# An RWKV block with FP4 feed-forward: the fifth branch's small products move beside two others, GpSimd's sums are split, and tiles are written in place

## Chip, cores, metric

One core of one Trainium2 chip. The metric is the device time of the kernel in microseconds, the median of three runs. The engines are TensorE (PE; its weight loads are PEld), VectorE (DVE), ScalarE (ACT), GpSimd (POOL), and SyncE (SP), which issues the DMAs.

## What is computed

The input is x of shape (2, 4096, 256), float32. A modulation vector gives scales, shifts and gates per batch. A layer norm with modulation leads into a two-layer RWKV-6 stack; its output, gated, is added to x; a second modulated layer norm leads into a feed-forward network with FP4-quantized weights and activations, gated and added again. The part that the change touches is the time mix of each layer:

```python
sx = _shift(x) - x
xxx = x + sx * p['x_maa']
mix = jnp.tanh(xxx @ p['tm_w1']).reshape(b * t, 5, E)                            # E = 32
mix = jnp.einsum('nfe,fed->fnd', mix, p['tm_w2']).reshape(5, b, t, d)
mw, mk, mv, mr, mg = mix
wx = x + sx * (p['w_maa'] + mw)     # and so for k, v, r and g
r = sigmoid(rx @ Wr); k = kx @ Wk; v = vx @ Wv; g = silu(gx @ Wg)
w = exp(-exp(time_decay + tanh(wx @ td_w1) @ td_w2))
# per head: out_t = r_t (S + u k_t v_t^T);  S = diag(w_t) S + k_t v_t^T
x = x + (groupnorm(out) * g) @ Wo
```

A channel mix follows (a shift, two interpolations, a squared ReLU and a sigmoid gate).

## The kernel before

**Tiles and steps.** All work is float32; a matmul of that type is two records in the trace, each with its own weight load. Time is cut into blocks of 256 positions. A step is one block of one batch in one layer: 2 batches x 2 layers x 16 blocks = 64 steps. Each (batch, layer) is a stream, a Python generator; the feed-forward's inputs, its chunks, its weights and the modulation are streams too.

**The planner.** The streams do not issue instructions. They record them with the class `Plan`, which simulates the five engines with a cost for each instruction and picks, again and again, the recorded instruction that could start first (with preferences for older work and for TensorE products that keep the array's form). What it picks is issued, so the order of every engine's queue is that of the plan, and the engines wait for each other by semaphores only. `Plan.after` says when a result is seen by the next engine: `LAT` of the producer plus `SEEN` of the consumer (55 ns for TensorE, 80 for GpSimd, 35 otherwise), or `SAME` on the same engine. `start` demands that all the PSUM banks that a group of products needs are free together; there are five banks, and the oldest group that still needs banks keeps as many from the others. The last lines of the kernel function make the plan for each of `PLANS` seeds (a jitter of the ages) without issuing, and then issue the one with the least planned end.

**Memory.** Work tiles come from stocks: `SLOTS` tiles of 514 floats per partition, `SLOTS2` double tiles of 1024 for the recurrence's r and k, `LONG` tiles of 768 for the feed-forward. A stream takes a tile from a stock and gives it back when it has recorded the last reader.

**Time mix.** `shifted` normalizes, transposes to channels by TensorE, scales into a second tile with one more column at the front (the last position of the block before), and lets GpSimd form the difference sx. The first product gives 128 rows for the branches w, k, v, r (32 each) and 128 more rows that hold the fifth branch's 32 rows four times, since the weights are laid out so. The second products have a contraction of 32: a product on rows 0 to 31 of the partitions uses row group 0 of the array, rows 32 to 63 group 1, and so on. The fifth branch uses groups 0 and 1, one for each block of 128 output channels, in two banks; then `branch_pair(0, 3)` (w and r) uses groups 0 and 3, and later `branch_pair(1, 2)` (k and v) groups 1 and 2. `to_input` empties a bank by two VectorE instructions, (product + maa) * sx, and one GpSimd sum adds x to the whole tile.

**The recurrence** (`wkv`) works on two chunks of 128 positions by seven levels of doubling. One stream at a time may record it (`head_lock`). It first writes copies of r and k, with the bonus u on even or odd positions, into two slots, for level 0; each level multiplies parts of r and k in place by products of the decays (`pair_view`).

Of the kernel before, what the change touches and what calls it, by code (L numbers as in the profile page):

```python
# [25 lines left out]
E = 32  # L26
# [11 lines left out]
TURNS = 30.0  # L38
SLOTS = 36
STAGGER = (12, 60)  # L40
PLANS, JITTER = 8, 8.0
SLOTS2 = 4
TINY = 16
LONG = 5
AHEAD_OPS = 24
# [72 lines left out]
class Plan:  # L118
# [10 lines left out]

    LAT = {"tensor": 170.0, "vector": 0.0, "scalar": 0.0, "gpsimd": 0.0, "sync": 2600.0, "load": 0.0}  # L130


    LAP = {"vector": 84.0, "scalar": 100.0, "gpsimd": 40.0}
    SEEN = {"tensor": 55.0, "gpsimd": 80.0}
    SAME = {"vector": 34.0, "scalar": 25.0, "gpsimd": 80.0}

# [323 lines left out]
def rwkv_adaln_fp4_kernel(ctx: ExitStack, tc: tile.TileContext, a: dict, out: bass.AP):  # L460
# [129 lines left out]
    for i in range(L):  # L590
        w = {}
        small = wp.tile([P, SMALL], F32, name=f"small{i}")
        load(small, a["small"][i])
        for n, v in enumerate(VECS):
            w[v] = small[:, n * J : (n + 1) * J]
        at = len(VECS) * J
        w["w1"] = small[:, at : at + J * 8 * E].rearrange("p (k n) -> p k n", k=J)
        at += J * 8 * E
        w["td1"] = small[:, at : at + J * ED].rearrange("p (k n) -> p k n", k=J)
        at += J * ED  # L600
        w2a, w["w2b"], w["td2"] = (small[:, at + m * D : at + (m + 1) * D] for m in range(3))
        w["w2"] = [w2a[E * f : E * (f + 1), :] for f in range(4)]
        for n in ("Wr", "Wk", "Wv", "Wg", "Wo"):
            w[n] = load_mat(f"{n}_{i}", a["L0_attn_" + n][i], J)
        w["wvm"] = const.tile([P, J * H], F32, name=f"wvm{i}")
        w["centred"] = False
        w["cWk"] = load_mat(f"cWk_{i}", a["L0_attn_cWk"][i], J)
        w["cWv"] = load_mat(f"cWv_{i}", a["L0_attn_cWv"][i], FD // P)
        w["cWr"] = load_mat(f"cWr_{i}", a["L0_attn_cWr"][i], J)
        lay.append(w)  # L610
        load_wmod(1 + i)
# [56 lines left out]
    for i in range(L):  # L668
        for b in range(B):
            nc.gpsimd.memset(state[i][b], 0.0)  # L670
            for m in range(2):
                nc.gpsimd.memset(carry[i][b][m], 0.0)
    diag = keep.tile([P, 2, C, J, 32], F32, name="diag")
    attn = keep.tile([P, 2, C, J, P], F32, name="attn")
# [83 lines left out]
    def shifted(h, ln_w, car):  # L758

        xn_s = take_slot()  # L760
        xn = v3(xn_s)
        yield from layernorm(h, xn)
        bk, pt = to_channels(xn)
        x_s = take_slot()
        xT = x_s.rearrange("p (j t) -> p j t", j=J)
        pl.vector.tensor_copy(xT[:, :, 0:1], car)
        for j in range(J):
            pl.scalar.activation(xT[:, j, 1:], pt[:, j, :], AF.Copy, scale=ln_w[:, j : j + 1])
        pl.close(bk)
        give(xn_s)  # L770
        pl.vector.tensor_copy(car, xT[:, :, TT : TT + 1])
        sx_s = take_slot()
        sx = v3(sx_s)
        pl.gpsimd.tensor_tensor(sx, xT[:, :, 0:TT], xT[:, :, 1:], ALU.subtract)
        yield
        return xT[:, :, 1:], sx, x_s, sx_s

    def lerp(x, sx, maa):
        m_s = take_slot()
        m = v3(m_s)  # L780
        for j in range(J):
            pl.vector.scalar_tensor_tensor(
                m[:, j, :], sx[:, j, :], maa[:, j : j + 1], x[:, j, :], ALU.mult, ALU.add
            )
        return m, m_s
# [18 lines left out]

    def pair_view(rk, h, n):

        v = rk[:, h : h + 1]
        return bass.AP(v.tensor, v.offset, [v.ap[0], [J * TT - h, 2], [2 * h, n], [1, h]])

# [27 lines left out]
    def wkv(i, b, rk_s, dec_s, v_s):  # L837

        S = state[i][b]
        rk = rk_s[:, : 2 * J * TT]  # L840
        r, k = (rk[:, m * J * TT : (m + 1) * J * TT].rearrange(
            "p (c j t) -> p c j t", c=C, j=J) for m in range(2))
        dec, v = v4(dec_s), v3(v_s)
        yield from take(head_lock, (i, b))
        late = pl.cur.late
        pl.cur.late = late - RUSH
        r0_s, k0_s = take_slot(), take_slot()
        r0, k0 = v4(r0_s), v4(k0_s)
        with_bonus(r0, r, 0, lay[i]["time_first"])
# [6 lines left out]
        tots_s = take_slot()  # L856
        at = 0
        def products(l):
            R, K = (r0, k0) if l == 0 else (r, k)
            wid = 64 if l == 6 else 32  # L860
# [16 lines left out]
        for l in range(7):  # L877
            h = 1 << l

            for m in {0: (), 1: (0, 1)}.get(l, (l,)):  # L880
                products(m)
            if l == 1:
                give(r0_s, k0_s)

# [3 lines left out]
            tv = tot.rearrange("p (n two) -> p n two", two=2)  # L888
            upd = pair_view(rk, h, n)
            pl.vector.tensor_tensor(  # L890
                upd, upd, tv.rearrange("p n m -> p m n").unsqueeze(3).to_broadcast([P, 2, n, h]), ALU.mult
            )
# [21 lines left out]
            yield  # L914
        give(dec_s)
        tot = tot.rearrange("p (c j) -> p c j", c=C)
        for q in range(4):
# [60 lines left out]
    def time_mix(i, b, h):  # L978
# [7 lines left out]
        for k in range(J):  # L986
            mm(pm[:, TT : 2 * TT], w["w1"][:, k, P:], xx[:, k, :], k == 0, k == J - 1)
        give(xx_s)
        mix_s = take_slot()
        mixa, mixb = mix_s[:, :TT], mix_s[:, TT : 2 * TT]  # L990
# [3 lines left out]

        def to_input(o, maa):

            m_s = take_slot()
            m = v3(m_s)
            for j in range(J):
                pl.vector.scalar_tensor_tensor(  # L1000
                    m[:, j, :], o[j], maa[:, j : j + 1], sx[:, j, :], ALU.add, ALU.mult
                )
            pl.gpsimd.tensor_tensor(m, m, x, ALU.add)
            return m_s

        def branch_pair(f, g, maa_f, maa_g):

            bks, os = zip(*(pl.bank() for _ in range(2)))
            for j in range(J):
                for e, o in zip((f, g), os):  # L1010
                    mm(
                        o[:, j * TT : (j + 1) * TT], w["w2"][e][:, j * P : (j + 1) * P],
                        mixa[E * e : E * (e + 1), :], True, True,
                    )
            ms = []
            for bk, o, maa in zip(bks, os, (maa_f, maa_g)):
                ms.append(to_input([o[:, j * TT : (j + 1) * TT] for j in range(J)], maa))
                pl.close(bk)
            return ms


        bks, os = zip(*(pl.bank() for _ in range(2)))
        for j in range(J):
            js = slice(j * E, (j + 1) * E)
            mm(os[j][:, :TT], w["w2b"][js, j * P : (j + 1) * P], mixb[js, :], True, True)
        xg_s = to_input([o[:, :TT] for o in os], w["g_maa"])
        for bk in bks:
            pl.close(bk)
        yield
        xw_s, xr_s = branch_pair(0, 3, w["w_maa"], w["r_maa"])  # L1030
        bk, pg = proj(w["Wg"], v3(xg_s))
        give(xg_s)
        g_s = take_slot()
        g_t = v3(g_s)
# [6 lines left out]
        for k in range(J):  # L1041
            for c in range(C):
# [3 lines left out]
                )  # L1046
        give(xw_s)
        td_s = take_slot()
        td = td_s[:, :P]
        pl.scalar.activation(td, pd[:, :P], AF.Tanh)  # L1050
        pl.close(bk)
        yield
        xk_s, xv_s = branch_pair(1, 2, w["k_maa"], w["v_maa"])
        give(mix_s, x_s, sx_s)
        rk_s = take_slot2()
# [31 lines left out]
        if not w["centred"]:  # L1087
# [8 lines left out]
            )  # L1096
        v_s = take_slot()
        xv = v3(xv_s)
        bk, o = proj_tok(w["Wv"], [xv[:, k, :] for k in range(J)])
        pl.scalar.copy(v3(v_s), o)  # L1100
        pl.close(bk)
        give(xv_s)
        yield

        o_s = yield from wkv(i, b, rk_s, dec_s, v_s)
        bk, pt = to_channels(v3(o_s))
        give(o_s)
        oT_s = take_slot()
        oT = v3(oT_s)
# [15 lines left out]
    def channel_mix(i, b, h):  # L1125
        w = lay[i]
        x, sx, x_s, sx_s = yield from shifted(h, w["ln2_w"], carry[i][b][1])
        xk, xk_s = lerp(x, sx, w["ck_maa"])
        xr, xr_s = lerp(x, sx, w["cr_maa"])
        give(x_s, sx_s)  # L1130
        yield
        kks = []
        for g in range(FD // P // 2):
            bk, o = pl.bank()
            o = halves(o)
            for m in range(2):
                n0 = (2 * g + m) * P
                for k in range(J):
                    mm(o[:, m, :], w["cWk"][:, k, n0 : n0 + P], xk[:, k, :], k == 0, k == J - 1)
            kks.append(take_slot())  # L1140
            kg = v3(kks[-1])
# [3 lines left out]
            yield  # L1145
        give(xk_s)
        sr_s = take_slot()
        sr = v3(sr_s)
        bk, o = proj_tok(w["cWr"], [xr[:, k, :] for k in range(J)])
        pl.scalar.activation(sr, o, AF.Sigmoid)  # L1150
        pl.close(bk)
        give(xr_s)
        yield
# [152 lines left out]
    def ffn_inputs():  # L1306
# [3 lines left out]
        for n in range(B * NT):  # L1310
# [5 lines left out]
            xn = v3(xn_s)  # L1316
            yield from layernorm_rows(x1, xn, rows["cb"][b], lambda c: rows["sb"][b])
            p_s = pl.take(long)
            yield from fp4(pl, xn_s, C * D, P, scales[0], p_s)
            long.append(p_s)  # L1320
            xq_s = take_slot()
            xqT = v3(xq_s)
            bk, pt = to_channels(xn)
            pl.scalar.copy(xqT, pt)
            pl.close(bk)
            give(xn_s)
            left = []
# [14 lines left out]
    def ffn_chunk(c, b, t, x1_s, xq_s, left):  # L1342
        HF = FI // 2
        cs_ = slice(c * P, (c + 1) * P)
        x1, xqT = v3(x1_s), v3(xq_s)
        hb_s = pl.take(long)
        hb = hb_s[:, :FI]
        for s in range(2):
# [12 lines left out]
            pl.close(bk)  # L1361
            yield
        p_s = pl.take(long)
        yield from fp4(pl, hb_s, FI, P, scales[1 + c], p_s)
        long.append(p_s)
        hT_s = pl.take(long)
        hT = hT_s.rearrange("p (f n) -> p f n", f=NF)
        for g in range(2):
# [8 lines left out]
            yield  # L1377
        long.append(hb_s)
        bk, y = pl.bank()
# [90 lines left out]
```

## Time and profile before

| | |
|---|---|
| runs of the kernel | 3128.61, 3125.28, 3124.25 us; median 3125.28 |
| profiled execution | 3123.61 us, span 3121.7 us, mean granted TensorE clock 0.981 |
| TensorE busy | 2984.9 us (96%), 38460 records |
| VectorE busy | 2365.4 us (76%) |
| ScalarE busy | 1615.4 us (52%) |
| GpSimd busy | 940.6 us (30%) |
| DMA | 42.53 MB, mean 14 GB/s |

Busy time of an engine is the time in which at least one of its instructions runs. In a group's row, the counts and shapes come first (output <- inputs, partitions x elements), then busy us and mean ns of one instruction, then the idle time of the engine just before them and what ended it. Nearly all instructions carry line 294, where the planner issues them, so groups are told apart by tiles and shapes. In the table of stretches the columns are: the stretch, its length, the busy us of PE, PEld, DVE, ACT and POOL, the granted clock, the DMA share and GB/s. In a row of waits: who waited, for whom, us in total, times, the longest.

### The profile page before, as it was taken

What the parts mean: (1) busy time and instruction counts of PE and PEld (TensorE: products, weight loads), DVE (VectorE), ACT (ScalarE), POOL (GpSimd) and SP (SyncE); (2) the same over time, 40 slices, a digit from 0 to 9 for tenths busy, and PEclk for the clock granted to TensorE, in tenths of its full rate; (3) what the DMA queues carried; (4) which work ended last, traced back from release to release, by engine and by line L of the source; (5) the groups of instructions that cost most, each with busy time, mean ns of one, the idle gap of its engine ahead of it and who ended that gap; (6) DMA issues with size and microseconds to landing.
All of it is one profiled execution on the core that took longest, in us unless ns stands there. A gap on an engine that the chain in (4) does not pass through costs nothing. (4 is left out here: it accounts for less than half of the span.)

```text
span 3121.7 us, 89338 instructions
## 1 busy us (share of the span) xinstructions
PE 2984.9 (96%) x38460; PEld 2412.9 (77%) x38460; DVE 2365.4 (76%) x6146; ACT 1615.4 (52%) x3362; POOL 940.6 (30%) x888
## 2 busy tenths in 40 slices
PE   6899999999999999999999999999999999999997
PEld 4777778778787777877778787787878778787775
DVE  6785778777877777778777787777777778766877
ACT  3565555545555556455454655546445455455442
POOL 2233323223233332332323233232332323331220
PEclk9899999999999999999999999999999999999989
DMA  4000000000000000000000000000000000000000
GB/s 141 20 14 5 10 7 15 7 15 7 9 12 7 16 8 11 11 6 17 5 11 11 5 18 5 14 8 9 13 6 17 5 8 15 9 9 9 8 13 11
DMA packets 35725, 42.53 MB, mean 14 GB/s; under 512 B 2817, under 2 KB 33537, under 8 KB 35329
## 3 DMA queue, kind: packets, MB, share of 16 engines
q1 hardware_dynamic: 35328, 36.81, 3.7%
q8 instruction: 302, 4.95, 0.7%
q14 instruction: 95, 0.77, 0.1%
HBM read 28.41 MB, written 8.39 MB: 12 GB/s over the span
## 5 line engine op out<-in xcount | busy, mean ns | idle before, releaser
L294 POOL TENSOR_TENSOR slot<-slot,slot 128x512 f32<-128x512 f32 (+1 forms) x448 | 508.9, 1152 | 961.5 <-DVE slot L294 682.0
L294 ACT ACTIVATE slot<-bank 128x512 f32<-128x512 f32 (+2 forms) x644 | 331.6, 519 | 682.8 <-PE bank L294 661.1
L294 POOL TENSOR_TENSOR tiny<-tiny,nhalf 128x2 f32<-128x2 f32 (+1 forms) x288 | 289.3, 1009 | 869.6 <-DVE tiny L294 789.4
L294 DVE TENSOR_TENSOR slot<-slot,slot 128x512 f32<-128x512 f32 x512 | 372.1, 728 | 110.2 <-PE pa L294 79.6
L294 PE MATMUL bank<-slot,small 32*128 32x256 f32 (+3 forms) x2816 | 393.3, 361 | 8.9 <-DVE slot L294 4.4
L294 PE MATMUL bank<-slot,cWk 128*128 128x256 f32 x1536 | 367.9, 385 | 2.5 <-DVE slot L294 2.0
L294 PE MATMUL bank<-cWv,slot 128*128 128x256 f32 x1536 | 343.8, 380 | 0.0
L294 PEld LDWEIGHTS pa<-slot 64*32 64x32 f32 x19456 | 224.0, 109 | 154.2 <-DVE diag L294 54.2
L294 PEld LDWEIGHTS bank<-slot,small 32*128 32x128 f32 (+3 forms) x2816 | 272.3, 178 | 88.3 <-issue 33.8
L294 PEld LDWEIGHTS bank<-slot,cWk 128*128 128x128 f32 x1536 | 284.5, 191 | 46.9 <-DVE slot L294 4.3
L294 PEld LDWEIGHTS bank<-cWv,slot 128*128 128x128 f32 x1536 | 289.2, 190 | 39.8 <-issue 0.3
L294 PE MATMUL pa<-slot 64*32 64x16 f32 x19456 | 266.2, 191 | 43.0 <-DVE diag L294 23.7
L294 ACT ACTIVATE slot<-bank,small 128x256 f32<-128x256 f32 (+1 forms) x640 | 248.4, 449 | 111.6 <-PE bank L294 109.9
L294 DVE SCALAR_TENSOR_TENSOR slot<-bank,small,slot 128x256 f32<-128x256 f32 x640 | 271.8, 473 | 24.9 <-PE bank L294 23.9
L294 DVE TENSOR_TENSOR slot<-slot,bank 128x512 f32<-128x512 f32 x192 | 131.0, 682 | 189.3 <-PE bank L294 143.0
L294 POOL TENSOR_TENSOR slot<-slot 128x512 f32<-128x512 f32 x128 | 141.9, 1111 | 346.8 <-ACT slot L294 272.3
L294 ACT ACTIVATE slot<-slot 128x512 f32<-128x512 f32 x288 | 181.3, 633 | 42.8 <-DVE slot L294 38.0
L294 DVE TENSOR_TENSOR long<-long,bank 128x352 f32<-128x352 f32 x256 | 131.1, 514 | 93.0 <-ACT long L294 69.8
L294 DVE SCALAR_TENSOR_TENSOR slot<-slot,small,slot 128x256 f32<-128x256 f32 x384 | 186.7, 518 | 16.8 <-POOL slot L294 16.7
L294 PE MATMUL bank<-ident,slot 128*128 128x128 f32 x1152 | 178.0, 283 | 14.0 <-ACT slot L294 8.6
L294 ACT COPY slot<-bank 128x512 f32<-128x512 f32 x224 | 130.3, 586 | 111.3 <-PE bank L294 107.3
L294 PE MATMUL bank<-wd,long 128*128 128x256 f32 x768 | 184.7, 391 | 1.2 <-ACT long L294 1.2
(106 smaller groups left out, 5362.5 us busy)
## 6 DMA issues: line engine op xcount, KB each, us to landing
slot<-in_L_attn_x_dram SPq DMA_DIRECT2D x64, 256.0 KB, 2.7
out_dram<-slot SPq DMA_DIRECT2D x64, 128.0 KB, 1.7
slot<-in_L_wmod_dram SPq DMA_DIRECT2D x6, 256.0 KB, 7.7
cWk<-in_L_attn_cWk_dram SPq DMA_DIRECT2D x2, 768.0 KB, 8.2
cWv<-in_L_attn_cWv_dram SPq DMA_DIRECT2D x2, 768.0 KB, 9.4
small<-in_small_dram SPq DMA_DIRECT2D x2, 718.0 KB, 8.3
long<-in_L_ffn_w_down_dram SPq DMA_DIRECT2D x2, 352.0 KB, 2.8
long<-in_L_ffn_w_gate_dram SPq DMA_DIRECT2D x5, 128.0 KB, 7.2
```

Source lines behind the costliest of these rows:

```text
L294: fn(*[real(v) for v in a], **{n: real(v) for n, v in k.items()})
```

## The change

The products: `branch_pair` becomes `branches`, which takes any number of branches and a place for each result. The fifth branch's two products use one bank and row group 1 (the second of its four copies), and stand in one group with those of w and r, in row groups 1, 0 and 3. The pair k and v stays.

```diff
-        w2a, w["w2b"], w["td2"] = (small[:, at + m * D : at + (m + 1) * D] for m in range(3))
-        w["w2"] = [w2a[E * f : E * (f + 1), :] for f in range(4)]
+        w2a, w2b, w["td2"] = (small[:, at + m * D : at + (m + 1) * D] for m in range(3))
+        w["w2"] = [w2a[E * f : E * (f + 1), :] for f in range(4)] + [w2b[E : 2 * E, :]]
...
-            pl.gpsimd.tensor_tensor(m, m, x, ALU.add)
+            for j in range(J):
+                pl.gpsimd.tensor_tensor(m[:, j, :], m[:, j, :], x[:, j, :], ALU.add)
...
-        def branch_pair(f, g, maa_f, maa_g):
-
-            bks, os = zip(*(pl.bank() for _ in range(2)))
+        def branches(es, places):
+
+            bks, os = zip(*(pl.bank() for _ in es))
             for j in range(J):
-                for e, o in zip((f, g), os):
+                for e, o in zip(es, os):
+                    rows_, mix = (slice(E * e, E * (e + 1)), mixa) if e < 4 else (slice(E, 2 * E), mixb)
                     mm(
-                        o[:, j * TT : (j + 1) * TT], w["w2"][e][:, j * P : (j + 1) * P],
-                        mixa[E * e : E * (e + 1), :], True, True,
+                        o[:, j * TT : (j + 1) * TT], w["w2"][e][:, j * P : (j + 1) * P], mix[rows_, :],
+                        True, True,
                     )
...
-        bks, os = zip(*(pl.bank() for _ in range(2)))
-        for j in range(J):
-            js = slice(j * E, (j + 1) * E)
-            mm(os[j][:, :TT], w["w2b"][js, j * P : (j + 1) * P], mixb[js, :], True, True)
-        xg_s = to_input([o[:, :TT] for o in os], w["g_maa"])
...
-        xw_s, xr_s = branch_pair(0, 3, w["w_maa"], w["r_maa"])
+        xg_s, xw_s, xr_s = branches((4, 0, 3), (None, None, None))
+        yield
...
-        xk_s, xv_s = branch_pair(1, 2, w["k_maa"], w["v_maa"])
-        give(mix_s, x_s, sx_s)
+        xk_s, xv_s = branches((1, 2), (None, sx_s))
+        give(mix_s, x_s)
+        while not stock2:
+            yield
```

GpSimd's sum of a branch becomes two instructions of 128x256, one for each block of channels (above). The recurrence's copies of r and k go into a fixed tile `rk2`, one for all streams; a table `place` names the tile that each level reads and writes (all `rk` but the first), and where two differ, ScalarE would copy the unchanged half:

```diff
+    rk2 = keep.tile([P, 2 * J * TT], F32, name="rk2")
...
-        r0_s, k0_s = take_slot(), take_slot()
-        r0, k0 = v4(r0_s), v4(k0_s)
+        r0, k0 = parts(rk2)
+        r, k = parts(rk)
...
+        place = {0: rk2, 1: rk, 2: rk, 3: rk, 4: rk, 5: rk, 6: rk, 7: rk}
...
+            here, there = place[l] if l else rk, place[l + 1]
+            if here is not there:
+                pl.scalar.copy(pair_view(there, h, n, False), pair_view(here, h, n, False))
```

Many results are written in place, over a tile whose last reader is the step that makes them: the scaled x over the normalized one in `shifted`, tanh over its input, g, the decay's hidden rows, v's branch (over sx), v, the transposed output, and in the channel mix and the feed-forward chunk likewise; for instance

```diff
-        x_s = take_slot()
+        x_s = xn_s
...
-        hT_s = pl.take(long)
+        hT_s = hb_s
```

The streams wait, while recording, until a long or a double tile is in the stock. The planner's numbers change as well:

```diff
-SLOTS = 36
+SLOTS = 37
...
-PLANS, JITTER = 8, 8.0
-SLOTS2 = 4
+PLANS, JITTER = 1, 8.0
+SLOTS2 = 3
...
-LONG = 5
+LONG = 4
...
-    LAT = {"tensor": 170.0, "vector": 0.0, "scalar": 0.0, "gpsimd": 0.0, "sync": 2600.0, "load": 0.0}
+    LAT = {"tensor": 170.0, "vector": 120.0, "scalar": 60.0, "gpsimd": 200.0, "sync": 2600.0, "load": 0.0}
...
-    SAME = {"vector": 34.0, "scalar": 25.0, "gpsimd": 80.0}
+    SAME = {"vector": 84.0, "scalar": 25.0, "gpsimd": 80.0}
```

More of the change, by code (lines that the diff above doesn't have):

```diff
@@ L769, in shifted @@
         pl.close(bk)
-        give(xn_s)
         pl.vector.tensor_copy(car, xT[:, :, TT : TT + 1])
@@ L776, in shifted, with lerp @@
         return xT[:, :, 1:], sx, x_s, sx_s
-    def lerp(x, sx, maa):
-        m_s = take_slot()
+    def lerp(x, sx, maa, m_s=None):
+        m_s = m_s or take_slot()
         m = v3(m_s)
@@ L803, in proj_tok, with parts, pair_view @@
         return bk, o
-    def pair_view(rk, h, n):
-        v = rk[:, h : h + 1]
-        return bass.AP(v.tensor, v.offset, [v.ap[0], [J * TT - h, 2], [2 * h, n], [1, h]])
+    def parts(rk):
+        return (
+            rk[:, m * J * TT : (m + 1) * J * TT].rearrange("p (c j t) -> p c j t", c=C, j=J) for m in range(2)
+        )
+    def pair_view(rk, h, n, changed=True):
+        v = rk[:, h : h + 1] if changed else rk[:, :1]
+        return bass.AP(
+            v.tensor, v.offset, [v.ap[0], [J * TT - h if changed else J * TT + h, 2], [2 * h, n], [1, h]]
+        )
     def with_bonus(dst, src, odd, u):
@@ L840, in wkv @@
         rk = rk_s[:, : 2 * J * TT]
-        r, k = (rk[:, m * J * TT : (m + 1) * J * TT].rearrange(
-            "p (c j t) -> p c j t", c=C, j=J) for m in range(2))
         dec, v = v4(dec_s), v3(v_s)
@@ L857, in wkv @@
         at = 0
+        place = {0: rk2, 1: rk, 2: rk, 3: rk, 4: rk, 5: rk, 6: rk, 7: rk}
         def products(l):
-            R, K = (r0, k0) if l == 0 else (r, k)
+            R, K = parts(place[l])
             wid = 64 if l == 6 else 32
@@ L881, in wkv @@
                 products(m)
-            if l == 1:
-                give(r0_s, k0_s)
             n = C * J * P // (2 * h)
             tv = tot.rearrange("p (n two) -> p n two", two=2)
-            upd = pair_view(rk, h, n)
+            here, there = place[l] if l else rk, place[l + 1]
+            if here is not there:
+                pl.scalar.copy(pair_view(there, h, n, False), pair_view(here, h, n, False))
             pl.vector.tensor_tensor(
-                upd, upd, tv.rearrange("p n m -> p m n").unsqueeze(3).to_broadcast([P, 2, n, h]), ALU.mult
+                pair_view(there, h, n), pair_view(here, h, n), tv.rearrange("p n m -> p m n").unsqueeze(3).to_broadcast([P, 2, n, h]), ALU.mult
             )
@@ L915, in wkv @@
         give(dec_s)
+        r, k = parts(rk)
         tot = tot.rearrange("p (c j) -> p c j", c=C)
@@ L987, in time_mix @@
             mm(pm[:, TT : 2 * TT], w["w1"][:, k, P:], xx[:, k, :], k == 0, k == J - 1)
-        give(xx_s)
-        mix_s = take_slot()
+        mix_s = xx_s
         mixa, mixb = mix_s[:, :TT], mix_s[:, TT : 2 * TT]
@@ L993, in time_mix, with to_input @@
         yield
-        def to_input(o, maa):
-            m_s = take_slot()
+        def to_input(o, maa, m_s=None):
+            m_s = m_s or take_slot()
             m = v3(m_s)
@@ L1002, in to_input @@
                 )
-            pl.gpsimd.tensor_tensor(m, m, x, ALU.add)
-            return m_s
-        def branch_pair(f, g, maa_f, maa_g):
-            bks, os = zip(*(pl.bank() for _ in range(2)))
+            for j in range(J):
+                pl.gpsimd.tensor_tensor(m[:, j, :], m[:, j, :], x[:, j, :], ALU.add)
+            return m_s
+        def branches(es, places):
+            bks, os = zip(*(pl.bank() for _ in es))
             for j in range(J):
-                for e, o in zip((f, g), os):
-                    mm(
-                        o[:, j * TT : (j + 1) * TT], w["w2"][e][:, j * P : (j + 1) * P],
-                        mixa[E * e : E * (e + 1), :], True, True,
+                for e, o in zip(es, os):
+                    rows_, mix = (slice(E * e, E * (e + 1)), mixa) if e < 4 else (slice(E, 2 * E), mixb)
+                    mm(
+                        o[:, j * TT : (j + 1) * TT], w["w2"][e][:, j * P : (j + 1) * P], mix[rows_, :],
+                        True, True,
                     )
             ms = []
-            for bk, o, maa in zip(bks, os, (maa_f, maa_g)):
-                ms.append(to_input([o[:, j * TT : (j + 1) * TT] for j in range(J)], maa))
+            for e, bk, o, s in zip(es, bks, os, places):
+                ms.append(to_input([o[:, j * TT : (j + 1) * TT] for j in range(J)], w["wkvrg"[e] + "_maa"], s))
                 pl.close(bk)
             return ms
-        bks, os = zip(*(pl.bank() for _ in range(2)))
-        for j in range(J):
-            js = slice(j * E, (j + 1) * E)
-            mm(os[j][:, :TT], w["w2b"][js, j * P : (j + 1) * P], mixb[js, :], True, True)
-        xg_s = to_input([o[:, :TT] for o in os], w["g_maa"])
-        for bk in bks:
-            pl.close(bk)
+        xg_s, xw_s, xr_s = branches((4, 0, 3), (None, None, None))
         yield
-        xw_s, xr_s = branch_pair(0, 3, w["w_maa"], w["r_maa"])
         bk, pg = proj(w["Wg"], v3(xg_s))
-        give(xg_s)
-        g_s = take_slot()
+        g_s = xg_s
         g_t = v3(g_s)
@@ L1046, in time_mix @@
                 )
-        give(xw_s)
-        td_s = take_slot()
+        td_s = xw_s
         td = td_s[:, :P]
@@ L1096, in time_mix @@
             )
-        v_s = take_slot()
+        v_s = xv_s
         xv = v3(xv_s)
@@ L1101, in time_mix @@
         pl.close(bk)
-        give(xv_s)
         yield
@@ L1106, in time_mix @@
         bk, pt = to_channels(v3(o_s))
-        give(o_s)
-        oT_s = take_slot()
+        oT_s = o_s
         oT = v3(oT_s)
@@ L1128, in channel_mix @@
         xk, xk_s = lerp(x, sx, w["ck_maa"])
-        xr, xr_s = lerp(x, sx, w["cr_maa"])
-        give(x_s, sx_s)
+        xr, xr_s = lerp(x, sx, w["cr_maa"], sx_s)
+        give(x_s)
         yield
@@ L1139, in channel_mix @@
                     mm(o[:, m, :], w["cWk"][:, k, n0 : n0 + P], xk[:, k, :], k == 0, k == J - 1)
-            kks.append(take_slot())
+            kks.append(take_slot() if g < FD // P // 2 - 1 else xk_s)
             kg = v3(kks[-1])
@@ L1145, in channel_mix @@
             yield
-        give(xk_s)
-        sr_s = take_slot()
+        sr_s = xr_s
         sr = v3(sr_s)
@@ L1151, in channel_mix @@
         pl.close(bk)
-        give(xr_s)
         yield
@@ L1317, in ffn_inputs @@
             yield from layernorm_rows(x1, xn, rows["cb"][b], lambda c: rows["sb"][b])
+            while not long:
+                yield
             p_s = pl.take(long)
@@ L1320, in ffn_inputs @@
             long.append(p_s)
-            xq_s = take_slot()
+            xq_s = xn_s
             xqT = v3(xq_s)
@@ L1325, in ffn_inputs @@
             pl.close(bk)
-            give(xn_s)
             left = []
@@ L1345, in ffn_chunk @@
         x1, xqT = v3(x1_s), v3(xq_s)
+        while not long:
+            yield
         hb_s = pl.take(long)
@@ L1362, in ffn_chunk @@
             yield
+        while not long:
+            yield
         p_s = pl.take(long)
@@ L1377, in ffn_chunk @@
             yield
-        long.append(hb_s)
         bk, y = pl.bank()
```

## The prediction

> **What bounds the kernel now.** I read the page first, then the busy time by stretches, then TensorE's waits, then its groups by shape, and last single runs of matmuls on the timeline.
>
> ```profile
> span 3121.7 us, 89338 instructions
> ...
> PE 2984.9 (96%) x38460; PEld 2412.9 (77%) x38460; DVE 2365.4 (76%) x6146; ACT 1615.4 (52%) x3362; POOL 940.6 (30%) x888
> ...
> PE   6899999999999999999999999999999999999997
> ```
>
> TensorE is busy nearly everywhere; VectorE is the next, with a quarter of the span free. The page's chain of waits ends after a few per cent of the span, so it is of no use here; the stretches are.
>
> ```profile
> 100.00:1000.00 900.00, 871.41 (x11634) 709.51 (x11634) 684.22 (x1829) 483.81 (x1018) 293.50 (x267) 0.99 0.04 10
> 1000.00:2000.00 1000.00, 972.34 (x13014) 789.95 (x13013) 760.71 (x1974) 540.83 (x1118) 305.53 (x285) 0.99 0.03 10
> 2000.00:2900.00 900.00, 882.75 (x11222) 713.31 (x11221) 683.66 (x1754) 467.44 (x974) 273.66 (x251) 0.99 0.03 10
> ```
>
> The first number after the length is TensorE's busy time: 2726.5 of 2800 us in the middle, so only 73.5 us idle there. The other 63 us of its 136.8 us idle lie in the first 100 us (34) and the last 222 us (30), at the weights' loading and the run-out. What it waits for in the middle:
>
> ```profile
> PE pa L294 <- DVE diag L294: 15.7, 29, 1.9
> PE bank L294 <- ACT slot L294: 12.6, 20, 1.7
> PE bank L294 <- DVE slot L294: 7.9, 14, 1.4
> PE bank L294 <- POOL slot L294: 7.0, 13, 1.4
> ```
>
> No wait is large. In this kernel TensorE's own work sets the time: less of it is a shorter span, as long as the new order leaves it no idler than now.
>
> **The second products.** Per step (64 steps: 2 batches, 2 layers, 16 blocks) the five branches take ten matmuls of 32 rows, each two records: two for the fifth, in row groups 0 and 1; four for w and r, in groups 0 and 3; four for k and v, in 1 and 2.
>
> ```profile
> L294 PE MATMUL bank<-slot,small 32*128 32x256 f32 x1280 | 181.6, 405 | 3.7 <-ACT slot L294 2.3 <-DVE slot L294 0.7 <-ACT long L294 0.3
> ```
>
> ```profile
> 218.94 0.70 PE L294 MATMUL bank<-slot,small 32*128 32x256 f32 x4
> ```
>
> ```profile
> 65.29 1.56 PE L294 MATMUL bank<-slot,small 32*128 32x256 f32 x12
> ```
>
> These are the fifth branch alone, and the fifth with w and r behind it. Record by record, from the first start of a run to the first start of what follows, the trace has 18 runs of 4 records (median 0.631 us), 74 of 8 (1.063), 40 of 12 (1.488), 6 of 20 (about 2.37) and one of 16 (about 2.2 without its waits). Each time is 0.43 us per product in the busiest row group, plus 0.20 us for changing the array's form and back. The run at 65.29 shows how: its records start at 0, 7, 20, 320, 327, 340, 536, 556, 752, 862, 967 and 1183 ns. Three start within 20 ns, so three row groups do run at once, and the run is long only because group 0 holds three products in turn: the fifth's and both of w's. After the change groups 1, 0 and 3 hold two each: four records in turn, like the run of 8, plus the 0.02 us by which the third starts later. So: before 18 x 0.631 + 74 x 1.063 + 40 x 1.488 + 6 x 2.37 + 2.2 = 166.0 us; after 64 x (1.083 + 1.063) = 137.3 us. Less by 28.7, call it 29 us. Should pairs of different streams meet as they do in the 7 longest runs, another 7 x 0.2 = 1.4 us goes. All of it is on TensorE, so on the path.
>
> The Trainium skill (TensorEngine Tiling (Array Packing), PSUM Bottleneck and Gotcha 1) speaks against this: row tiles need a PSUM bank each and speed TensorE up, but not the emptying of banks. If emptying bounded the group, the triple would cost six evictions of 0.474 us, 2.84 instead of 1.08 us: by this estimate 64 x 1.76 = 113 us more, and a time near 3208.
>
> The row is this:
>
> ```profile
> L294 DVE SCALAR_TENSOR_TENSOR slot<-bank,small,slot 128x256 f32<-128x256 f32 x640 | 271.8, 473 | 24.9 <-PE bank L294 23.9
> ```
>
> Their number, 640, stays, and one bank per step fewer is taken (the fifth used two halves). All TensorE waits on VectorE's slots in the middle are 7.9 us. I take 0 for the emptying; its upper bound is in the second rival.
>
> **A cover that goes.** In the code order w's and r's products stood between the fifth's and Wg, which needs the fifth's sum. That sum comes after two evictions, the handover (0.08 us to GpSimd in the trace) and 1.20 us of GpSimd: 0.95 + 0.08 + 1.20 = 2.2 us, of which the pair hid up to 1.06 and other streams the rest.
>
> ```profile
> L294 PE MATMUL bank<-slot,Wg 128*128 128x256 f32 x512 | 127.2, 392 | 6.8 <-POOL slot L294 6.0 <-ACT long L294 0.4 <-ACT slot L294 0.4
> ```
>
> The rest, 1.1 us x 64 = 73 us, cost 6.0 us of waits: other streams filled 92% of it. Another 1.06 x 64 = 68 us to be filled costs 8% of that, 5 us. From below it is 0 (streams fill all), from above 68 (none). I take 5, since the same wait at the same place is the nearest row.
>
> **GpSimd's sums.** Five per step become ten of half the size: 320 of 1201 ns go, 640 come. The nearest row is the output's sum.
>
> ```profile
> L294 POOL TENSOR_TENSOR slot<-slot,slot 128x512 f32<-128x512 f32 x384 | 454.8, 1201 | 801.5 <-DVE slot L294 529.9 <-ACT slot L294 184.0 <-issue 36.0
> ...
> L294 POOL TENSOR_TENSOR slot<-slot,slot 128x256 f32<-128x256 f32 x64 | 54.6, 853 | 160.0 <-DVE slot L294 152.1 <-DVE tiny L294 3.4 <-PE bank L294 3.2
> ```
>
> 640 x 0.853 - 320 x 1.201 = +162 us on an engine that is idle for 2181. The first half may start after one eviction, and the last ends 0.35 us sooner behind the second; in a burst of three branches GpSimd is the slower (6 x 0.85 = 5.1 against 3 x 1.2 = 3.6 us), so r's input comes up to 1.5 us later, behind Wg (8 records at 0.216 = 1.7 us) and other work. On the path: between -7 us (every TensorE wait on GpSimd in the middle gone) and +7 (doubled); I take 0. VectorE may be held up a little more by GpSimd: its 128x512 products of two SBUF tiles have a median of 0.685 us with no GpSimd work beside them and a mean of 0.83 to 0.86 with. That is at most some 10 us on an engine with 756 us to spare: 0.
>
> **Factors, tiles, waits.** The adapted r and k go into one fixed tile instead of two rotating slots: the same four ScalarE instructions, and the written-out copy never occurs since all places are the same tile. The recurrence is entered by one stream at a time, so the first products on that tile are long done. Writing in place adds only waits for readers whose result the writer needs anyway, except the 0.18 us column copy in the shift, now behind the transposes and beside two 0.5 us ScalarE scalings. Three of the double tiles instead of four, with a wait in the generator (no instruction): counted from the start of each Wr group to the end of its state update, the trace never has four in flight and three for only 114 us. Fewer long tiles: a chunk needs two at a time instead of three, two chunks fit. All 0.
>
> **The order.** One plan is made instead of the best of eight, and its waiting times grow by 120, 60 and 200 ns after VectorE, ScalarE and GpSimd. In the trace a consumer starts 0.03 (ScalarE), 0.055 (TensorE) or 0.08 us (GpSimd) after its producer's end, which is what the present numbers say; the new ones overstate it. But a planned wait is not executed: only the order changes. No row of before prices another order. It can give back at most the 73.5 us; it can lose as much if it doubles them. I take 0, for want of a sign, and keep about half of each for the range.
>
> **Sum.** The profiled execution took 3123.6 us (span 3121.7 and 1.9 around it). 3123.6 - 29 + 5 = 3099.6; the median of the runs, 3125.28, stands 1.7 above the profiled one: 3101.
>
> **Rivals.**
> *1. The order eats it.* The plan without a choice leaves 18 to 30 us more idle, a quarter to two fifths of the middle's idle: 3119 to 3131, no change (about 0.2%, 6.3 us, is what can be told from none). For: eight against one. Against: nothing in the trace shows the choice was worth that.
> *2. Slower: three banks at once.* The triple starts only when three of the five banks are free, and while it is the oldest such work it keeps three from the others. Then it holds them for six evictions of 0.474 us, 2.84 us, while TensorE has two: 0.9 us of work if they get transposes, 3.5 if projections. A wait of 0 to 1.9 us, 0.95 in the mean, x 64 = 61 us: 3101 + 61 = 3162. It decides from 24/64 = 0.38 us per step. For: VectorE, 76% busy, is in order. Against: the 7.9 us above, and in runs of 20 records three groups already met without much of a wait.
> *3. The order gains.* More slots, and margins that fit the spread of VectorE's and GpSimd's durations, take 30 us or more of the middle's 73.5: 3050 to 3070.
> *4. It does not run three abreast.* The offsets at 65.29 speak against it; then only the 21 or so saved form changes count (139 runs to about 118), 4 us: 3124.
>
> **How the numbers follow.** Forecast (3072 to 3118) 0.52; gain in the order 0.09; eaten or not abreast 0.14; three banks or a worse order, above 3131, 0.25. So faster 0.62 with a little of the third, same 0.13, slower 0.25. From 3068 to 3150 some 0.8 is held: 0.08 lies below, 0.12 above.
>
> **What would show it.** Right: the 32-row group falls from 181.6 to about 150 us busy, with runs of 12 records at 1.08 us; TensorE's idle in the middle stays within 60 to 90 us; GpSimd near 1100 us. Wrong: 12 records at 1.49 us (not abreast); TensorE waiting on VectorE's slots by 40 us or more (banks); Wg waiting on GpSimd by 20 us or more (cover); or idle and form changes spread over all groups (order).

## The result, and the profile after

The changed kernel takes 3112.86 us (median of six runs, 3109.37 to 3117.74) against 3125.01 for the kernel before beside it: a ratio of 0.9956, 95% interval 0.9943 to 0.9969. That is faster by 0.44%, about 12 us, where 24 were forecast. The profiled execution took 3109.37 us, 14.2 less than that of before, its span 3107.5.

The page, the same three rows as before:

```profile
span 3107.5 us, 89878 instructions
...
PE 2954.6 (95%) x38460; PEld 2393.5 (77%) x38460; DVE 2342.9 (75%) x6146; ACT 1618.7 (52%) x3368; POOL 1014.5 (33%) x1208
...
PE   6899999999999999999999999899999999999997
```

TensorE is busy for 30.3 us less, but the span is shorter by 14.2 only: its idle time rose from 136.8 to 152.9. The stretches say where (PE's busy time is the first number after the length):

```profile
100.00:1000.00 900.00, 868.81 (x11482) 710.62 (x11481) 684.71 (x1835) 485.73 (x1018) 315.03 (x375) 0.98 0.04 11
1000.00:2000.00 1000.00, 965.91 (x13025) 785.50 (x13023) 746.94 (x1976) 535.32 (x1117) 335.19 (x389) 0.99 0.03 10
2000.00:2900.00 900.00, 873.28 (x11428) 711.39 (x11427) 683.75 (x1774) 482.39 (x996) 295.71 (x343) 0.99 0.03 10
```

2708.0 of 2800 us: 92.0 idle in the middle, against 73.5. All of the new idle time, and a little more, lies there; the first 100 us and the run-out hardly changed. The waits of TensorE in the middle, longest first:

```profile
PE pa L294 <- DVE diag L294: 19.4, 29, 2.2
PE bank L294 <- ACT slot L294: 14.1, 20, 1.5
PE bank L294 <- DVE slot L294: 13.1, 17, 3.6
PE pa L294 <- DVE slot L294: 9.9, 11, 1.9
PE bank L294 <- POOL slot L294: 8.4, 9, 4.0
PE pa L294 <- ACT attn L294: 6.2, 10, 1.5
```

The six longest rows are all longer than before, by 1.4 to 5.3 us; none makes up the 18.5 alone. All waits before the recurrence's products (`pa`) together rose from 29.4 to 42.5 us, those before products into banks from 38.1 to 45.5. The second products and Wg, by shape, and a triple on the timeline:

```profile
L294 PE MATMUL bank<-slot,small 32*128 32x256 f32 x1280 | 146.9, 400 | 3.0 <-ACT slot L294 2.5 <-issue 0.3 <-DVE slot L294 0.2
...
L294 PE MATMUL bank<-slot,Wg 128*128 128x256 f32 x512 | 127.2, 392 | 4.2 <-POOL slot L294 2.9 <-POOL tiny L294 1.2
```

```profile
64.28 1.14 PE L294 MATMUL bank<-slot,small 32*128 32x256 f32 x12
```

The group fell by 34.7 us. All 64 triples run three abreast: 12 records in 1.070 us (median to the start of what follows), where 12 took 1.488. TensorE's work falls into 1195 stretches of one form of the array instead of 1229. Of the work that went, 32.7 us lie in this group when each record is counted up to the next one's start and time at half clock as half; the rest is spread over the other groups, none of which changed by more than 1.8.

One more term can be read from the trace's clock records. The granted clock is either full or half, and a time at half clock lasts 3.41 us or, less often, a few times that. Before, TensorE was busy for 97.5 us at half clock, so that 48.7 us of its busy time are slowness; after, 114.9 and 57.5. So the difference of the two profiled executions is: work at full clock -39.1 (2936.2 to 2897.1), clock +8.8, idle +16.1, sum -14.2.

### The profile page after: what moved, and what is told of

Its sections match the earlier page's. It is cut to its first block, busy times and chain, and to the rows that moved or that the text cites. A ratio compares the mean times of both kernels' runs of the same rounds, so it can differ in the third digit from the quotient of the medians.

```text
span 3107.5 us, 89878 instructions
## 1 busy us (share of the span) xinstructions
PE 2954.6 (95%) x38460; PEld 2393.5 (77%) x38460; DVE 2342.9 (75%) x6146; ACT 1618.7 (52%) x3368; POOL 1014.5 (33%) x1208
## 4 chain that ended last, share of the span: by engine, by line
PE 44%; DVE 8%; ACT 4%; issue 1%; POOL 0%; POOLq 0%; DVEq 0%; ACTq 0%
PE bank L294 40%; DVE slot L294 4%; PE pa L294 4%; ACT slot L294 2%; DVE long L294 2%; ACT attn L294 1%; DVE tiny L294 1%; ACT L294 1%; DVE scales L294 1%; PE kv L294 1%; ACT rk L294 1%; DVE diag L294 1%; DVE S L294 0%; POOL tiny L294 0%; POOL slot L294 0%
## 5 line engine op out<-in xcount | busy, mean ns | idle before, releaser
L294 POOL TENSOR_TENSOR slot<-slot,slot 128x256 f32<-128x256 f32 (+1 forms) x768 | 575.8, 776 | 845.7 <-DVE slot L294 620.8
L294 POOL TENSOR_TENSOR tiny<-tiny,nhalf 128x2 f32<-128x2 f32 (+1 forms) x288 | 297.3, 1035 | 897.3 <-DVE tiny L294 874.7
L294 PE MATMUL bank<-slot,small 32*128 32x256 f32 (+3 forms) x2816 | 359.1, 359 | 4.7 <-ACT slot L294 3.1
L294 PEld LDWEIGHTS pa<-slot 64*32 64x32 f32 (+1 forms) x19456 | 224.2, 109 | 159.7 <-DVE diag L294 53.0
L294 PE MATMUL pa<-slot 64*32 64x16 f32 (+1 forms) x19456 | 266.2, 191 | 47.9 <-DVE diag L294 22.9
L294 PEld LDWEIGHTS bank<-slot,small 32*128 32x128 f32 (+3 forms) x2816 | 248.5, 178 | 76.7 <-issue 33.0
L294 ACT ACTIVATE slot<-slot,tiny 128x256 f32<-128x256 f32 x256 | 143.3, 596 | 107.6 <-DVE tiny L294 104.5
L294 PE MATMUL bank<-ident,slot 128*128 128x128 f32 x1152 | 176.5, 280 | 13.8 <-ACT slot L294 10.6
```

Of the source, the lines that this page charges most:

```text
L294: fn(*[real(v) for v in a], **{n: real(v) for n, v in k.items()})
```

## The experiments

TensorE has 39 us less work at full clock, and the profiled execution is 14 us shorter. The question was where the other 25 us went: to a wait that the parts of the change make (banks, GpSimd, the lost cover), or to another order of the queues. In the kernel before, the choice among eight seeds takes seed 0, which is also what is taken without a choice; in the changed kernel it would take seed 6. So the seed can be pinned, and some edits can be made with every engine's order left as it was. Ratios are to the kernel before, run on the same chip beside each.

**Row groups 1 and 2, order of before.**

```diff
-            js = slice(j * E, (j + 1) * E)
+            js = slice((1 + j) * E, (2 + j) * E)
```

> The kernel before, in the same order of instructions on every engine; only the fifth branch's two products use row groups 1 and 2 instead of 0 and 1, so that no group holds three products in the runs of 12 records. Theory P (TensorE's work is the time, and less of it passes through when the order stays): the 40 runs of 12 records fall from 1.488 to about 1.07 us, TensorE's busy time falls by 40 x 0.42 = 17 us, and the time falls by 13 to 17 us, to about 3109. Rival V (VectorE's emptying of the banks or GpSimd's sums set the pace behind these products): TensorE's busy time falls as said, its idle time grows by as much, and the time stays within 4 us of 3125.

Measured: 0.9982 (0.9972 to 0.9991), so 5.6 us faster. TensorE's busy time fell by 13.0 us, its idle time rose by 7.9, the span fell by 5.1: between the two theories. TensorE's row, the products' row, and Wg's behind them:

```profile
PE 2971.9 (95%) x38460; PEld 2398.4 (77%) x38460; DVE 2365.8 (76%) x6146; ACT 1615.8 (52%) x3362; POOL 941.4 (30%) x888
...
L294 PE MATMUL bank<-slot,small 32*128 32x256 f32 x1280 | 167.8, 406 | 4.6 <-ACT slot L294 2.6 <-DVE slot L294 0.9 <-ACT long L294 0.7
L294 PE MATMUL bank<-slot,Wg 128*128 128x256 f32 x512 | 131.7, 403 | 9.3 <-POOL slot L294 8.9 <-ACT long L294 0.4
```

The products became 13.8 us shorter and Wg's wait 2.5 us longer. What stands next in TensorE's queue was put there for a product that ended later, and often is not ready: from the start of a run of 12 records to the next start it is 1.075 us at best, but 1.343 in the median of the 40, and 18 of them are followed by idle time.

**The same question with a larger lever: the triple lengthened, order of seed 6.**

```diff
-rows_, mix = (slice(E * e, E * (e + 1)), mixa) if e < 4 else (slice(E, 2 * E), mixb)
+rows_, mix = (slice(E * e, E * (e + 1)), mixa) if e < 4 else (slice(0, E), mixb)
```

The weights of the fifth branch are taken from rows 0 to 31 accordingly.

> The changed kernel in the order of seed 6, the same order on every engine; only the fifth branch's products use row group 0, where w's stand, instead of group 1. Group 0 then holds four products in turn and the triple takes 1.92 instead of 1.07 us: 64 x 0.86 = 55 us more on TensorE, and nothing else. Theory P (TensorE's work is the time): TensorE's busy time grows by 55 us and the time by 45 to 60 us, from 3074 to about 3125. Rival V (what follows the triple waits for VectorE and GpSimd anyway; when the order stays, as with row groups 1 and 2, only a third to a half passes through): 15 to 30 us, 3089 to 3104.

Measured: 0.9935 (0.9922 to 0.9948), against 0.9817 for the same order with three abreast. In the profiles (the first row of the second view is that of three abreast, the other that of the lengthened triple):

```profile
PE 2994.0 (96%) x38460; PEld 2443.8 (79%) x38460; DVE 2364.3 (76%) x6146; ACT 1583.7 (51%) x3340; POOL 1031.6 (33%) x1208
```

```profile
L294 PE MATMUL bank<-slot,small 32*128 32x256 f32 x1280 | 149.4, 400 | 4.8 <-DVE slot L294 2.9 <-ACT slot L294 1.5
...
L294 PE MATMUL bank<-slot,small 32*128 32x256 f32 x1280 | 199.8, 402 | 1.7 <-ACT slot L294 1.5
```

The lengthened runs take 1.919 us, as expected. The products grew by 50.4 us, all of TensorE's busy time by 56.0, the span by 36.4, since idle time fell by 19.6. So with the order kept 65% of the added busy time pass through to the span, and the rest is time in which TensorE would have waited. Part of this is the clock: 56.9 us instead of 41.3 were lost at half clock. Without the clock it is 20.8 of 40.4 us, about half; with row groups 1 and 2 it was 5.1 of 13.0, and 4.2 of 12.0 without the clock. By the ratios the lengthened triple costs 37 us, between P's 45 to 60 and V's 15 to 30. So P as it was written (all passes) is wrong; a third to two thirds pass through, and two single pairs of profiles give no sharper number.

**Orders alone.** Nothing but the seed is changed in these:

```diff
-    best = min(range(PLANS), key=lambda seed: plan(seed, True))
+    best = 1
```

> The kernel before with the plan of seed 1; seed 0 is the one that the choice among eight takes in it, so the choice is what this run takes away. Nothing else differs. Theory P (the change lost in the order what it lacks of its forecast): an order that was not picked out costs 10 to 25 us, all of it in TensorE's idle time and changes of form: 3135 to 3150. Rival V (orders are alike on the chip; the change's loss is a wait that its own parts make): 3120 to 3130.

Measured: 1.0093 (1.0078 to 1.0109), 29 us slower, more than either theory expected. The profiled execution is 47.4 us longer than that of before: 25.5 more idle, 13.9 more lost at half clock, 8.0 more work at full clock. All of the new idle time lies at the end, where the last streams run out one by one:

```profile
2900.00:3169.10 269.10, 211.22 (x1635) 162.48 (x1633) 190.05 (x418) 87.29 (x173) 43.27 (x43) 0.90 0.03 9
```

57.9 us idle against 29.4 in the kernel before; in the middle it is 71.8, no more than before. So this order costs idle time in another place than the changed kernel's 18.5 us in the middle.

> The changed kernel with the plan of seed 1 instead of seed 0; both are taken without a choice. Theory P: another ordinary order, 3105 to 3125 (the spread between orders). Rival V: the same as seed 0 within 4 us, 3109 to 3117.

Measured: 0.9984 (0.9976 to 0.9993), 5 us faster than before and 9 us slower than the changed kernel with seed 0.

> The changed kernel with the plan of seed 6, which a choice among eight by the planned end would take. Theory P: with a picked order the products' whole saving shows, 28 to 32 us below the kernel before: 3093 to 3098. Rival V: the loss belongs to the parts and stays, 3109 to 3117.

Measured: 0.9817 (0.9804 to 0.9831), 57 us faster than the kernel before, more than the products can give and below the ranges of both theories.

```profile
PE 2938.0 (96%) x38460; PEld 2389.6 (78%) x38460; DVE 2358.7 (77%) x6146; ACT 1583.7 (52%) x3340; POOL 1033.6 (34%) x1208
```

Against the changed kernel with seed 0: idle 132.8 instead of 152.9, 41.3 instead of 57.5 us lost to the clock, 1149 stretches of one form instead of 1195; the work at full clock is the same within half a us (2896.7 and 2897.1). So the same code in three orders takes 0.9817, 0.9956 and 0.9984 of the time before, 52 us apart: the order alone moves this kernel by more than the change's own 12 us, and rival V, by which orders are alike and the loss is a fixed wait of the parts, fails in all three runs. What is not shown is how the 16 us of new idle time divide. With the order kept, a third to two thirds of TensorE's saved work come back as idle time, which for 39 us is 13 to 26 and would by itself be enough.

**The split sums alone, order of before.** The two halves are issued inside one planned instruction:

```diff
             pl.gpsimd.tensor_tensor(m, m, x, ALU.add)
+            op = pl.cur.queue[-1]
+            op.calls = [
+                (op.calls[0][0], (m[:, j, :], m[:, j, :], x[:, j, :], ALU.add), {}) for j in range(J)
+            ]
```

> The kernel before in the same order; each of the five sums of a step is issued as two halves inside one planned instruction, so that nothing but the split differs. Theory P (the split lies beside TensorE's work): GpSimd's busy time grows by 100 to 160 us, TensorE's waits on GpSimd change by less than 7 us, the time stays within 6 us of the kernel before. Rival S (VectorE and GpSimd hold each other up): VectorE's 128x512 products get slower and the time grows by over 8 us.

Measured: 0.9997 (0.9987 to 1.0007), no difference. GpSimd's busy time rose by 59 us only (940.6 to 999.6), since a half takes less than the output's sum:

```profile
L294 POOL TENSOR_TENSOR slot<-slot,slot 128x256 f32<-128x256 f32 x704 | 486.0, 716 | 675.6 <-DVE slot L294 656.3 <-DVE tiny L294 13.6 <-DVE scales L294 1.4
```

VectorE's 128x512 products have a mean of 725 ns against 728. This run also shows what the clock does by itself: same order, idle 135.0 against 136.8 us, yet its profiled span is 9.4 us longer, because 61.0 instead of 48.7 us were lost at half clock. The clock's 8.8 us in the comparison above are within that, so the two profiles alone do not show them to be the change's. The mean granted clocks of all runs say more: 0.976 to 0.978 in the six runs of the changed kernel, 0.977 to 0.983 in the 47 runs of the kernel before beside the experiments (their means by chip 0.979 to 0.981), and 0.973 to 0.977 and 0.981 to 0.985 in the changed kernel with seeds 1 and 6. So the clock seems to go with the order, and by an estimate (the difference of the means times the span) some 5 to 11 us of the changed kernel's time are owed to it. TensorE's wait at Wg halved here, from 6.8 to 3.4 us, with every order kept:

```profile
L294 PE MATMUL bank<-slot,Wg 128*128 128x256 f32 x512 | 129.0, 396 | 3.4 <-POOL slot L294 2.4 <-ACT long L294 0.4 <-ACT slot L294 0.4
```

**The other parts, one at a time,** each in the order that a choice among eight takes for it. Here the order differs along with the part.

> The changed kernel with the fifth branch's products as before (row groups 0 and 1, two banks, ahead of w and r), in the order that a choice among eight takes for it (seed 1). Against the changed kernel in its chosen order (seed 6). Theory P (three abreast saves 30 us of TensorE's work, whatever the order): 3095 to 3110, with 22 to 32 us more in the 32-row group. Rival B (taking three banks at once costs the order what the array saves): within 12 us of seed 6, 3062 to 3086.

The triple undone:

```diff
-        xg_s, xw_s, xr_s = branches((4, 0, 3), (None, None, None))
-        yield
+        bks, os = zip(*(pl.bank() for _ in range(2)))
+        for j in range(J):
+            js = slice(j * E, (j + 1) * E)
+            mm(os[j][:, :TT], w["w2b"][js, j * P : (j + 1) * P], mixb[js, :], True, True)
+        ...
+        xw_s, xr_s = branches((0, 3), (None, None))
```

Measured: 0.9874 (0.9858 to 0.9889), 18 us behind seed 6 of the changed kernel. The 32-row group has 178.7 us (29.3 more), but idle time is 119.1 instead of 132.8. By the ratio it is 3086 (0.9874 x 3125), the very end of B's range and short of P's; but 18 us are also more than the 12 by which B has it, so neither is borne out.

> The kernel before with the triple alone, in the order that a choice among eight takes for it (seed 6). Theory O (two thirds of the products' 29 us pass through, as when the order of seed 6 was kept and the products lengthened, and the order that goes with them is as good or bad as it falls): 3085 to 3125. Rival B (three banks at once spoil the order where the tiles give the planner less room): 3130 or more.

The triple alone, in the kernel before. Measured: 1.0040 (1.0025 to 1.0055), slower. Its work at full clock is 31.9 us less than before's (2904.3 against 2936.2), but idle time is 177.1 us, 100.4 of it in the middle, and now Wg does wait:

```profile
L294 PE MATMUL bank<-slot,Wg 128*128 128x256 f32 x512 | 130.3, 399 | 12.0 <-POOL slot L294 11.9
```

That is rival B's result. It is one order, though, and another order alone cost the kernel before 29 us; so it shows that the triple is not safe by itself, not that banks are the reason. TensorE's wait on VectorE's slots in the middle is 14.8 us against 7.9.

> The kernel before with the triple, the split sums and the new waiting times of the planner, but with the tiles as before (no writing in place, r and k copies in two slots, the old stocks), in the order that a choice among eight takes for it (seed 2). Theory P (tiles cost and bring nothing but another order): like the changed kernel in its chosen order within the spread between chosen orders, 3065 to 3095. Rival T (the tiles are what lets the planner look ahead, and the gain of the chosen order over the kernel before is theirs): 3105 to 3130.

Measured: 0.9934 (0.9918 to 0.9951); 148.2 us idle. By the ratio that is 3104, above P's range and just below T's, and within what one order differs from another.

> The changed kernel with the planner's waiting times of before (LAT, SAME), in the order that a choice among eight takes for it (seed 4). Theory O (the waiting times act only as another order): within the spread between chosen orders, 3060 to 3095. Rival M (the added waiting times are a margin that makes an order hold on the chip): 3105 to 3130.

```diff
-    LAT = {"tensor": 170.0, "vector": 120.0, "scalar": 60.0, "gpsimd": 200.0, "sync": 2600.0, "load": 0.0}
+    LAT = {"tensor": 170.0, "vector": 0.0, "scalar": 0.0, "gpsimd": 0.0, "sync": 2600.0, "load": 0.0}
```

(`SAME` likewise.) Measured: 0.9953 (0.9936 to 0.9969), 159.6 us idle: M's range. The last run below, also without the margins, contradicts M.

**A planner that knows the triple's price.** Each second product was planned at 0.57 of a full one. With

```diff
+            pl.cur.last.cost = 2 * 432.7
             ms = []
```

> The changed kernel with the planner told what the second products take in the trace (two slots of 0.433 us for the triple as for the pair, instead of 0.57 of a full product for each), in the order with the least planned end among 24 seeds (seed 18). Theory O (a picked order carries over to the chip, and the planner's right price for the triple helps a little): 3050 to 3080. Rival N (the planned end tells the chip's order apart no better than chance): 3090 to 3125.

Measured: 0.9900 (0.9879 to 0.9921), 3094 by the ratio: N's lower end, 144.4 us idle.

> The same with the planner's waiting times of before, the least planned end among 20 seeds (seed 18). Theory O: 3045 to 3080, as the kernel with the right price alone. Rival N: 3090 to 3125.

Measured: 0.9823 (0.9799 to 0.9847), 134.1 us idle in the profiled execution (which lost only 20.0 us to the clock and was the shortest of its runs). By the ratio it is 3070, in O's range, where the run before it was in N's. So two kernels are 1.8% faster than the kernel before and 1.3 to 1.4% faster than the changed one: the changed kernel in the order of seed 6, and this one. They cannot be told apart.

The price and the waiting times change nothing but the plan. So the changed kernel's instructions have been run in six orders: two taken without a choice (0.9956, 0.9984) and four with the least planned end of eight or more (0.9817, 0.9823, 0.9900, 0.9953). The chosen ones are on average 30 us faster, though the slowest of them is no better than seed 0.

## Why the prediction was half right

**Three row groups at once: right, and to size.** 1.070 us measured for 1.083 worked out from the offsets of a single run; the 32-row group 146.9 us for "about 150". The work at full clock fell by 39.1 us, ten more than the sum's 29, with 34 fewer changes of form; 32.7 of it are the group's, the other 6.4 were not forecast. That the result lies within 3072 to 3118 is partly luck. In the profiles 39.1 less work and 16.1 more idle time make 23.0, close to the 24 forecast only because two errors cancel, and the clock, for which the sum has no term, takes 8.8; the gain is half of the forecast, and the range holds it by its margin for the order.

**"All of it is on TensorE, so on the path": wrong in size.** This is the step that failed. 97% busy was read as 97% bound. The two runs with the order kept show 39% (5.1 of 13.0) and 65% (36.4 of 56.0) passing through, 35% and 51% without the clock. A reading that fits, and is argued: TensorE's next products wait for evictions and sums that do not get faster with it, and the 74 us of idle time are only the part of these near misses that is visible now. At a third to two thirds, 29 us would have been 10 to 19.

**The order at 0: mis-sized, with a share that stays open.** The prediction kept about half of 73.5 us, some 37, for it, but the value was 0. Six orders of the changed kernel lie 52 us apart. Without a choice (seeds 0 and 1) it has 153 and 163 us idle, in its chosen order 133; the kernel before has 137 in its chosen order and 162 with seed 1. The prediction asked for a row that prices another order, found none, and should have asked what the choice had been among: the kernel before stood at a chosen order, and in the few orders tried the chosen ones are the faster on average. This speaks for rival 1, which had 18 to 30 us more idle; 18.5 came in the middle. But the same idle time follows from the step above, so how much of it is the order's is open. Putting the choice back gives 43 us (0.9956 to 0.9817), 16 of them at the clock in the profiles.

**The cover: hidden behind the halves.** 5 us were added for Wg's wait; it fell from 6.8 to 4.2. The run with the split alone and the order kept shows why it could: the halves bring it to 3.4 without the triple. With the triple it is longer: 12.0 without the halves, and with them 4.2 and 5.7 in the changed kernel's seeds 0 and 6, against 1.0 with the triple undone. These orders differ, so the triple's share is argued; but it fits the 5 us, and the halves, for which the sum took 0, take off 3.4.

**Emptying the banks.** TensorE's wait on VectorE's slots in the middle rose from 7.9 to 13.1 us, but not at the triple: the second products wait 0.2 us for them. The growth is at the channel mix's first product, which waits for its input:

```profile
L294 PE MATMUL bank<-slot,cWk 128*128 128x256 f32 x1536 | 367.9, 385 | 2.5 <-DVE slot L294 2.0 <-DVE long L294 0.5
...
L294 PE MATMUL bank<-slot,cWk 128*128 128x256 f32 x1536 | 373.7, 389 | 9.6 <-DVE slot L294 9.6
```

The first row is the kernel before, the second the changed one; with seed 1 the kernel before has 7.3, so an order alone can make it. The Trainium skill (TensorEngine Tiling (Array Packing), PSUM Bottleneck) says that emptying may become the limit; here it did not, and the 113 us that it would have made, or the 61 of rival 2, did not come.

**GpSimd.** +162 us were expected of it, +73.9 came (1014.5): the row that was taken as nearest, the output's sum at 853 ns, is dearer than a half at 723. That it costs TensorE nothing was right: with the order kept the time is the same within some 4 us.

**Tiles and planned waiting times at 0: open.** TensorE's wait at the recurrence's first products, which read the new fixed tile, is 4.6 us (4.1 before), so this tile at least costs nothing. The runs that undo the tiles and the waiting times differ from the chosen order by 37 and 42 us, but so do orders among each other (0.9817 to 0.9984 for one code), and with the right price the kernel without the margins is as fast as any. To settle it would take many seeds of each.

**In the list of what would show it,** TensorE's idle time in the middle was to stay within 60 to 90 us; it is 92.0. Of the line for the order, "idle and form changes spread over all groups", the idle time came true; the changes of form became fewer.

## What to carry to other kernels

Where a program is laid out by a planner, any edit draws a new order, and one order of the same code differs from another by more (here 1.7%) than a good edit brings: compare versions each at its best of several measured orders, or keep the order and change one thing. An engine that is 97% busy is not 97% bound: shorten or lengthen its work with the order kept to see what share passes through (here a third to two thirds) before the whole of a saving is put into a sum.

## What the runs showed of the hardware

Products of 32 rows in different row groups run independently even when they are not neighbours in the queue: in the run at 65.29 us of the kernel before, r's first product in group 3 started 20 ns after the fifth branch's, ahead of w's, which stand first in the code and waited for group 0. The records do not name the group; it is read from their starts, which follow each other by 0.22 to 0.32 us within a group.

TensorE's clock falls to one half (128x256 products then start every 427 instead of 216 ns) for 3.41 us or a few times that, and in the middle of the span (twelve such places in the kernel before) it does so without any single idle stretch of TensorE over 2.5 us; 0.4 to 2.6 us of idle time lay in the 3.41 us ahead of each. The Trainium skill (TensorE: Matmul & The Clock Gate, Part 1) has the same stretch, 3413 ns, and the same half. Its rule is no idle gaps beyond about 3.4 us; it also tells of a kernel whose clock swings through short idle times between groups of matmuls, without a number for them. The places here are of this second kind. The kernel before lost 48.7 us of busy time to it on top of 136.8 us idle. How much is lost does not simply follow the idle time: the run with the least idle time, the lengthened triple's 113.3 us, lost 56.9, and the last one 20.0 with 134.1. And it is not the same in each execution: between two with one order and nearly the same idle time it differed by 12 us.
